# Four gate products of the feed-forward moved across a step boundary in a macaron block

## The chip, the cores and the metric

The kernel runs on one core of one Trainium2 chip. The metric is the device time of one execution in microseconds; the median of several executions is compared. A profile of one execution is read beside it. PE is TensorE, PEld its weight loads, DVE is VectorE, ACT is ScalarE, POOL is GpSimd and SP is SyncE, which issues nearly all DMAs.

## The reference

A macaron block over x of shape (4, 1024, 512): half a feed-forward, a selective-scan layer, half a feed-forward with the same weights, each on a layer norm of its input and added to it.

```python
x = x + 0.5 * ffn(layernorm(x))
x = x + attn(layernorm(x))
x = x + 0.5 * ffn(layernorm(x))

def ffn(x):                       # gate_w, up_w: 1408 x 512, down_w: 512 x 1408
    g = (x @ gate_w.T) * gate_s
    u = (x @ up_w.T) * up_s
    return (silu(g) * u) @ down_w.T * down_s

def attn(x):                      # 1024 channels, 16 states each
    h, gate = split(W_in @ x.T)
    h = silu(conv4(h) + conv_b)
    ts, Bm, Cm = split(h.T @ Wx.T)          # 128, 16, 16; each rms-normed
    delta = softplus(Wdt @ ts + dt_bias)
    # per channel and state: s = exp(delta * A) * s + delta * B * h;  y = sum_n s * C
    return ((y + D * h) * silu(gate)) @ Wout.T
```

All arithmetic is float32.

## The kernel before

The 4096 rows of x are 32 tiles of 128 rows. The scan layer works in sixteen steps, k = 0 to 15, of 256 positions (two tiles). Four steps make one of the four sequences. Beside the scan of a step, its "background" does three other things: a feed-forward over three or four row tiles (some of the first feed-forward, some of the second, by the table BESIDE), the output projection of the step before, and the input projection, convolution and scan parameters of the step after. A front part before step 0 and an end part after step 15 do the rest.

The numbers of tiles by step are 3, 3, 4, 4, 3, 4, 4, 3, 4, 4, 3, 4, 4, 3, 3, 3. So a step with three is followed by a step with four at k = 1, 4, 7 and 10.

**The scan.** A step has 32 units, `unit(k, i, g)`: eight channel blocks i by four groups g of states. "Unit i" of a step is written below for the four groups of block i. In a unit, ACT computes exponentials into PSUM (`da`, L573, two instructions for each of two halves), POOL the product with B (`sb`, L576), DVE the recurrence (L580) and the product with C (L590). PE sums over the states with a folding matrix (`yps`, L602), one block later; these sums free the 14 buffers of `sb`. The exponentials use `rep`, a copy of delta and delta times h that is spread over partitions through two DMAs (`rows`, `spread`). Before a pair of blocks, `head` computes delta: PE forms `dp` (L490), ACT takes its absolute value, relu, exponential and logarithm (`z`, `lg`, L498 to L503), and POOL completes `dd`. Its parts are popped as "chores" inside the units.

**The feed-forward of a step.** `FFN.flip` transposes a normalised tile on PE (`tpf`, L235) and ACT copies it to `fxT` (L238). `gate()` has eleven parts; a part has four matmuls against one 256 KB weight tile (`gate_w`, L273) and a copy to `hd` on ACT (L287). After parts 3, 7 and 10 a silu runs over the copies so far (L199), with a load of its function table ahead of it and another after it. `up()` has eleven parts of the same matmuls, which DVE multiplies into `hd` (L304). `down()` has one part for each tile, eleven matmuls of 512 columns (`fo`, L319), which DVE adds to the tile (`xf`, L327). `hd` and `fxT` have one buffer each.

**The order.** `background(k)` (L704) writes the parts in a list: loads, statistics, then gate and up parts as a rhythm between which the gate projection of the scan (`gp`, L545), transposes, the output projection (`op`, L633), the convolution (`hp`, L376) and the parameters (`sp`, `t`, then `tsT`, L455) stand, and at the end the transposes of the next step's feed-forward between the down parts. Each part is a `Work` with a cost for PE and one for DVE. The main loop emits a unit and then as many parts as keep the shares of both costs level with the units (`total` and `total_v` are sums over the step's list):

```python
while parts and (
    done * total_v < vector * total
    or (length - len(parts)) * (units - HEAD) < upto * min(n, units - HEAD)
):
    c, v = step()
    done, vector = done + c, vector + v
```

The second condition has the parameters of the next step ready eleven units before the end (HEAD). A scheduler may still reorder instructions a little when the program is built, except where the code pins the order.

Weight tiles are fetched in the order of the parts, twelve ahead (LEAD), into a ring of fourteen; all of them and the scan's DMAs go through SP's queue.

Of the kernel before, what the change touches and what calls it, by code (L numbers as in the profile page):

```python
# [25 lines left out]
NCS = B * CPB  # L26
# [7 lines left out]
HALVES = 14  # L34
LEAD = 12
FRONT = 5
RING = 14

BESIDE = [(3, 0), (3, 0), (2, 2), (2, 2), (1, 2), (2, 2), (2, 2), (2, 1), (2, 2), (2, 2), (2, 1), (2, 2), (2, 2), (1, 2), (0, 3), (0, 3)]
# [3 lines left out]
def macaron_kernel(ctx: ExitStack, tc: tile.TileContext, a: dict, out: bass.AP):  # L43
# [8 lines left out]
    p8 = ctx.enter_context(tc.tile_pool(name="p8", bufs=8))  # L52
    ring = ctx.enter_context(tc.tile_pool(name="ring", bufs=RING))
    dram = ctx.enter_context(tc.tile_pool(name="scratch", bufs=1, space=bass.MemoryType.DRAM))
# [109 lines left out]
    def settle():  # L164
        while deferred:
            deferred.pop(0)[1]()
# [20 lines left out]
    def then(f, *args):  # L187
        return Work(0, 0, lambda: f(*args))
# [54 lines left out]
    class FFN:  # L243
# [35 lines left out]
        def gate(self):  # L279
            self.done = 0  # L280

            def part(it):
                def emit(w):
                    if it == 0:
                        self.hd = p1.tile([P, NF, 2 * T], F32, tag="hd", name=f"hd{self.name}")
                    gp = self.product("gate_w", it, w[0])
                    nc.scalar.activation(  # L287
                        self.hd[:, it, : self.n], gp, AF.Copy, scale=gate_s[:, it : it + 1]
                    )
                    if it % 4 == 3 or it == NF - 1:  # L290
                        h = self.hd[:, self.done : it + 1, : self.n]
                        silu(h)
                        self.done = it + 1

                return Work(KH * self.n, 0, emit, [("gate_w", it)], settled=it == 0)

            return [part(it) for it in range(NF)]
# [69 lines left out]
    def prep_conv(k):  # L367
        def part(i):
            def emit(w):
                if i == 0:  # L370
                    st[k]["u"] = p2.tile([P, NI, T], F32, tag="u", name=f"u{k}")
                u = st[k]["u"]
                hp = ps_m.tile([P, 512], F32, tag="mm", name=f"hp{k}_{i}")
                w = cols(w[0])
                for kk in range(KH):
                    nc.tensor.matmul(  # L376
                        hp[:, : K - 1 + T], lhsT=w[:, kk, :], rhs=st[k]["xnT"][:, kk, :],
                        start=(kk == 0), stop=(kk == KH - 1),
                    )
                nc.scalar.activation(  # L380
                    u[:, i, :], hp[:, 0:T], AF.Identity,
                    bias=conv_b[:, i : i + 1], scale=conv_w[:, i, 0:1],
                )

                def taps():
                    for q in range(1, K):
                        pin(nc.vector.scalar_tensor_tensor(  # L387
                            u[:, i, :], hp[:, q : q + T], conv_w[:, i, q : q + 1], u[:, i, :],
                            ALU.mult, ALU.add,
                        ))  # L390
                    if i == NI - 1:
                        defer(1, lambda: silu(u))

                defer(1, taps)

            return Work(KH * T, 4 * T, emit, [("W_in", i)], settled=i == 0)

        return [part(i) for i in range(NI)]
# [223 lines left out]
    def tail(k):  # L622

        wo = []

        def part(j):
            def emit(w=None):
                wo.extend(w or [])
                assert all(("gated", i) in st[k] for i in range(NI))
                x = st[k]["xo", j]  # L630
                op = ps_m.tile([P, H], F32, tag="mm", name=f"op{k}_{j}")
                for i in range(NI):
                    nc.tensor.matmul(  # L633
                        op, lhsT=st[k]["u"][:, i, j * P : (j + 1) * P], rhs=wo[i],
                        start=(i == 0), stop=(i == NI - 1),
                    )
                nc.vector.tensor_tensor(x, x, op, ALU.add)
                if k + 1 < NCS:
                    store(x2[k * J + j], x)

            return Work(NI * H, H, emit, [("Wout", i) for i in range(NI)] if j == 0 else (), settled=j == 0)

        r = [part(j) for j in range(J)]
        r[0].until = r[-1]
        return r

    def weave(xs, by):

        r = []
        for n, w in enumerate(xs):  # L650
            r.append(w)
            r += by[n : n + 1]
        return r, by[len(xs) :]

    def flips(f, prep):

        seq = [(f, t) for t in range(len(f.tiles))] if f else []
        if prep is not None:
            seq += [(None, j) for j in range(J)]
        xn = {}  # L660

        def begin(n):
            if n < len(seq):
                of, t = seq[n]
                xn[n] = of.stats(t) if of else prep_stats(prep, t)

        def start():
            begin(0)
            begin(1)

        def part(n):
            def emit():
                of, t = seq[n]
                if of:
                    of.flip(xn[n], t)
                else:
                    prep_flip(prep, t, xn[n])
                begin(n + 2)

            return Work(KH * P, H if n + 2 < len(seq) else 0, emit)  # L680

        return [Work(0, 2 * H, start)] + [part(n) for n in range(len(seq))]
# [13 lines left out]
    ffn = {k: FFN(k, beside[k]) for k in range(NCS)}  # L696
# [7 lines left out]
    def background(k):  # L704

        f = ffn[k]
        prep = k + 1 if k + 1 < NCS else None
        gates, out_of = gate(k), tail(k - 1) if k else []
        turn = flips(None, prep) if prep is not None else []
        conv = params = []  # L710
        if prep is not None:
            conv, params = prep_conv(prep), prep_params(prep)
            ready[k] = params[-1]
        parts = [then(tail_load, k - 1)] if k else []
        if prep is not None:
            parts.append(then(prep_load, k + 1))
        parts += turn[:1]
        p = [NOTHING] * (4 if k else 0) + gates + turn[1:] + out_of + conv
        tiles = (f.gate() if k else []) + f.up()
        p = [p[n : n + 2] for n in range(0, len(p), 2)]  # L720
        p += [[NOTHING]] * 4 + [[w] for w in params]
        turn = flips(ffn[k + 1], None) if k + 1 < NCS else []
        for n, w in enumerate(tiles):
            parts.append(w)
            for q in p[n : n + 1]:
                parts += q
            if n == len(tiles) - NF and k + 1 < NCS:
                parts.append(then(ffn[k + 1].load))
            if n == len(tiles) - NF and k + 1 == NCS:
                parts.append(then(tail_load, k))  # L730
                parts.append(then(end_load))
            if n == len(tiles) - 2:
                parts += turn[:1]
        for q in p[len(tiles):]:
            parts += q
        w, turn = weave(turn[1:2] + f.down(), [NOTHING] + turn[2:])
        return parts + w + turn

    ready = {}


# [5 lines left out]
    front += [turn_f[0]] + weave(prep_conv(0), [down[3]] + turn_f[1:])[0]  # L747
    front += weave(gate_0[:FRONT], prep_params(0))[0]
    beside_scan = [background(k) for k in range(NCS)]
    end = FFN("e", last)  # L750
    turn = flips(end, None)
    back_end = tail(NCS - 1) + turn + end.gate() + end.up() + end.down()
    for w in front + gate_0[FRONT:] + [w for b in beside_scan for w in b] + back_end:
        if w.blocks:
# [8 lines left out]
    settle()  # L763
    between = gate_0[FRONT:]
    chores = head(0, 0)
# [16 lines left out]
    for k in range(NCS):  # L782
        more = k + 1 < NCS
        parts, n, done, vector = list(beside_scan[k]), 0, 0, 0
# [121 lines left out]
```

## Time and profile before

| | us |
|---|---|
| median of 3 executions | 3239.61 (3236.33 to 3240.49) |
| the profiled execution | 3238.13 |
| its span, first to last instruction | 3236.4 |
| front part, to the first exponential of step 0 | 200.5 |
| steps 1, 4, 7, 10 (three tiles, before four) | 192.7, 175.9, 178.7, 186.2 |
| steps 2, 5, 8, 11 (four tiles, after three) | 183.1, 182.4, 181.6, 181.9 |
| steps 3, 6, 9, 12 (four tiles, after four) | 185.0, 186.2, 186.3, 186.2 |
| end part, from the end of step 15's scan | 134.4 |

A page of the profile gives the busy time of each engine, groups of equal instructions, and the chain of work that ended last. Each view can be asked for a window of the span. The table cuts the span where the first exponential of a step starts on ACT; PE and DVE may be a little ahead of or behind this cut. In a line, "out<-in" are tiles by their names in the program, "x" is a count of instructions, and a bracket has the idle time before it and who ended it. A float32 matmul appears as two records, so a gate product of four matmuls has eight. PEclk is the granted share of PE's clock.

### The profile page before, as it was taken

The numbers are of one execution on the slowest core, as the hardware profiler recorded it, in microseconds if no ns is written. First come the engines' busy times: TensorE is split into PE (matmuls) and PEld (weight loads), VectorE is DVE, ScalarE is ACT, GpSimd is POOL, SyncE is SP. The second block draws the span as 40 slices with busy tenths as digits, with TensorE's granted clock in tenths as the row PEclk, the third lists the DMA queues.
The fourth block names the chain that finished last, engine by engine and source line by source line (L and its number), as shares of the span: only waits on it lengthen the run. The fifth ranks groups of instructions, "written<-read, shape, count | busy, mean of one in ns | idle before, by whom it ended". The sixth has DMA issues, their size and how long they took to land.

```text
span 3236.4 us, 41939 instructions
## 1 busy us (share of the span) xinstructions
PE 3057.3 (94%) x12448; PEld 1648.5 (51%) x12448; DVE 2475.0 (76%) x4981; ACT 1787.2 (55%) x3535; POOL 1937.9 (60%) x1895
## 2 busy tenths in 40 slices
PE   8988898999999999999999999989999998989999
PEld 3554453545555454545545554645555554554434
DVE  1259788888969898787979798787969788788831
ACT  3265564747556664746565564747556474655430
POOL 0066857566675757566765767576665756667510
PEclk9999998999999999999999999999999999999999
DMA  5364554646566555546565655655565654646531
GB/s 169 113 170 118 172 171 135 178 120 199 138 186 175 171 167 160 171 122 209 136 180 163 182 157 162 187 133 171 153 177 162 172 171 135 179 117 195 143 97 43
DMA packets 287426, 506.43 MB, mean 156 GB/s; under 512 B 32096, under 2 KB 50272, under 8 KB 287200
## 3 DMA queue, kind: packets, MB, share of 16 engines
q1 hardware_dynamic: 285616, 503.31, 54.7%
q8 instruction: 100, 1.64, 0.2%
q14 instruction: 126, 1.03, 0.1%
q10 hardware_dynamic: 1584, 0.45, 0.1%
HBM read 442.03 MB, written 61.60 MB: 156 GB/s over the span
## 4 chain that ended last, share of the span: by engine, by line
PE 61%; DVE 20%; ACT 8%; POOL 5%; issue 4%; DMA 1%; SPq 0%; ACTq 0%; DVEq 0%; POOLq 0%
PE fo L319 13%; PE gate_w L273 12%; DVE da L580 12%; PE up_w L273 7%; PE hp L376 5%; PE yps L602 5%; PE gp L545 5%; PE op L633 4%; DVE sb L590 4%; ACT da L573 3%; POOL sb L576 2%; PE gate_wp L273 1%; PE dp L490 1%; PE gate_we L273 1%; PE foe L319 1%
## 5 line engine op out<-in xcount | busy, mean ns | idle before, releaser
L576 POOL TENSOR_TENSOR sb<-rep,bc 128x512 f32<-128x512 f32 x1024 | 1275.4, 1273 | 450.1 <-PE yps L602 378.5
L580 DVE TENSOR_TENSOR_SCAN da<-da,state,sb 128x256 f32<-128x256 f32 x1536 | 1055.9, 737 | 284.4 <-ACT da L573 250.3
L573 ACT ACTIVATE da<-rep,a_w 128x256 f32<-128x256 f32 x2048 | 899.1, 471 | 537.3 <-DVE sb L590 521.7
L590 DVE TENSOR_TENSOR sb<-da,bc 128x512 f32<-128x512 f32 x1024 | 686.1, 677 | 0.9
L273 PE MATMUL gate_w<-fxT,w_gate_w 128*128 128x384 f32 (+1 forms) x1408 | 565.8, 549 | 5.6 <-ACT dd L499 2.3
L273 PE MATMUL up_w<-fxT,w_up_w 128*128 128x384 f32 (+1 forms) x1408 | 564.5, 551 | 0.8 <-issue 0.4
L319 PE MATMUL fo<-w_down_w,hd 128*128 128x512 f32 x1232 | 546.5, 598 | 0.0
L602 PE MATMUL yps<-sb,fold 128*32 128x256 f32 x4096 | 320.0, 393 | 84.0 <-DVE sb L590 75.3
L273 PEld LDWEIGHTS up_w<-fxT,w_up_w 128*128 128x128 f32 x1408 | 267.0, 194 | 249.5 <-issue 157.1
L273 PEld LDWEIGHTS gate_w<-fxT,w_gate_w 128*128 128x128 f32 x1408 | 267.3, 193 | 247.0 <-issue 151.3
L580 DVE TENSOR_TENSOR_SCAN da<-da,sb 128x256 f32<-128x256 f32 x512 | 320.4, 677 | 85.4 <-ACT da L573 66.0
L319 PEld LDWEIGHTS fo<-w_down_w,hd 128*128 128x128 f32 x1232 | 231.4, 192 | 273.1 <-issue 264.0
L521 POOL TENSOR_SCALAR e<-z 128x512 f32<-128x512 f32 x64 | 124.3, 1942 | 276.1 <-ACT z L502 252.1
L602 PEld LDWEIGHTS yps<-sb,fold 128*32 128x32 f32 x4096 | 125.9, 110 | 281.3 <-DVE sb L590 133.5
L376 PE MATMUL hp<-mxT,w_W_in 128*128 128x259 f32 x1024 | 243.6, 390 | 24.4 <-issue 13.0
L545 PE MATMUL gp<-mxT,w_W_in 128*128 128x256 f32 x1024 | 241.3, 385 | 2.9 <-ACT dd L499 1.8
L376 PEld LDWEIGHTS hp<-mxT,w_W_in 128*128 128x128 f32 x1024 | 193.9, 192 | 82.8 <-issue 34.2
L633 PE MATMUL op<-w_Wout,u 128*128 128x512 f32 x512 | 225.0, 595 | 4.6 <-issue 2.9
L545 PEld LDWEIGHTS gp<-mxT,w_W_in 128*128 128x128 f32 x1024 | 193.6, 191 | 60.7 <-issue 17.9
L287 ACT ACTIVATE hd<-gate_w,gate_s 128x384 f32<-128x384 f32 (+1 forms) x176 | 110.5, 629 | 166.2 <-PE gate_w L273 165.3
L387 DVE SCALAR_TENSOR_TENSOR u<-hp,conv_w,u 128x256 f32<-128x256 f32 x384 | 177.1, 473 | 17.4 <-ACT u L380 14.6
L304 DVE SCALAR_TENSOR_TENSOR hd<-up_w,up_s,hd 128x384 f32<-128x384 f32 (+1 forms) x176 | 117.2, 666 | 59.9 <-PE up_w L273 59.8
(112 smaller groups left out, 2654.2 us busy)
## 6 DMA issues: line engine op xcount, KB each, us to landing
rep<-row SPq DMA_DIRECT2D x512, 256.0 KB, 5.1
w_W_in<-in_W_in_dram SPq DMA_DIRECT2D x256, 256.0 KB, 3.4
w_gate_w<-in_gate_w_dram SPq DMA_DIRECT2D x198, 256.0 KB, 3.9
w_up_w<-in_up_w_dram SPq DMA_DIRECT2D x198, 256.0 KB, 3.2
w_down_w<-down_w SPq DMA_DIRECT2D x187, 256.0 KB, 2.8
row<-dd SPq DMA_DIRECT2D x128, 256.0 KB, 3.2
w_Wout<-in_Wout_dram SPq DMA_DIRECT2D x128, 256.0 KB, 3.4
bc<-bcd SPq DMA_DIRECT2D x64, 256.0 KB, 4.7
```

Source lines behind the costliest of these rows:

```text
L273: nc.tensor.matmul(o[:, : self.n], lhsT=w[:, k, :], rhs=self.xT[:, k, : self.n], start=(k == 0), stop=(k == KH - 1),)
L319: nc.tensor.matmul(op, lhsT=self.hd[:, it, t * P : (t + 1) * P], rhs=wd[it], start=(it == 0), stop=(it == NF - 1),)
L376: nc.tensor.matmul(hp[:, : K - 1 + T], lhsT=w[:, kk, :], rhs=st[k]["xnT"][:, kk, :], start=(kk == 0), stop=(kk == KH - 1),)
L387: pin(nc.vector.scalar_tensor_tensor(u[:, i, :], hp[:, q : q + T], conv_w[:, i, q : q + 1], u[:, i, :], ALU.mult, ALU.add,))
L521: lambda: pin(nc.gpsimd.tensor_scalar(e, z, 1.0, 1.0, ALU.add, ALU.subtract)),
L545: nc.tensor.matmul(gp[:, :T], lhsT=w[:, kk, :], rhs=st[k]["xnT"][:, kk, K - 1 :], start=(kk == 0), stop=(kk == KH - 1),)
L573: nc.scalar.activation(da[:, j, :], rep[:, h + j, 0, :], AF.Exp, scale=a_w[:, b0 + h + j, g : g + 1])
L576: nc.gpsimd.tensor_tensor(sb, rep[:, hs, 1, :], d["bc"][:, g : g + 1, :].to_broadcast([P, 2, T]), ALU.mult)
L580: nc.vector.tensor_tensor_scan(da[:, j, :], da[:, j, :], sb[:, j, :], 0.0 if first else state[:, b0 + h + j, g : g + 1], ALU.mult, ALU.add,)
L590: nc.vector.tensor_tensor(sb, da, d["bc"][:, NS + g : NS + g + 1, :].to_broadcast([P, 2, T]), ALU.mult)
L602: nc.tensor.matmul(yp[j * Q : (j + 1) * Q, :], lhsT=fold, rhs=pr[j // 2][:, j % 2, :], start=(g == 0), stop=(g == NS - 1),)
L633: nc.tensor.matmul(op, lhsT=st[k]["u"][:, i, j * P : (j + 1) * P], rhs=wo[i], start=(i == 0), stop=(i == NI - 1),)
```

## The change

At the end of the list of step k, if step k has fewer feed-forward tiles than step k+1, the first four gate parts of step k+1 are appended; step k+1 starts with the other seven. This holds at k = 1, 4, 7 and 10. Step 0 and the last are left out by the condition. The moved parts are the same instructions with the same weight loads; the costs that the planner sums up move with them from one step to the other.

```diff
+EARLY = 4
...
     def background(k):
...
-        tiles = (f.gate() if k else []) + f.up()
+        tiles = (begun.pop(k) if k in begun else f.gate() if k else []) + f.up()
...
         w, turn = weave(turn[1:2] + f.down(), [NOTHING] + turn[2:])
-        return parts + w + turn
-
+        parts += w + turn
+        if 0 < k < NCS - 1 and len(f.tiles) < len(ffn[k + 1].tiles):
+            gates = ffn[k + 1].gate()
+            parts += gates[:EARLY]
+            begun[k + 1] = gates[EARLY:]
+        return parts
+
+    begun = {}
     ready = {}
```

## The prediction, made before the changed kernel ran

> **What bounds the kernel now.** I read the page's busy times first, then cut the span into the sixteen scan steps (a step has 128 of the 2048 exponentials of L573; it starts with its first), then followed the chain of waits through steps 4 and 5, then the waits behind it.
>
> Busy times on the page:
>
> ```profile
> PE 3057.3 (94%) x12448; PEld 1648.5 (51%) x12448; DVE 2475.0 (76%) x4981; ACT 1787.2 (55%) x3535; POOL 1937.9 (60%) x1895
> ```
>
> The windows of steps 4, 5, 10 and 11 (start:end us, length, then busy us and instructions of PE, PEld, DVE, ACT, POOL, then PEclk, the DMA share and GB/s):
>
> ```profile
> 914.20:1090.10 175.90, 167.12 (x777) 97.67 (x775) 146.61 (x325) 110.00 (x224) 122.49 (x119) 0.99 0.65 184
> 1090.10:1272.50 182.40, 176.96 (x715) 94.38 (x716) 155.56 (x323) 107.52 (x214) 120.49 (x119) 0.99 0.55 154
> ...
> 2005.30:2191.50 186.20, 171.11 (x775) 98.50 (x773) 154.52 (x328) 110.89 (x224) 121.66 (x119) 0.96 0.61 173
> 2191.50:2373.40 181.90, 176.80 (x714) 94.28 (x715) 152.97 (x262) 107.43 (x214) 119.70 (x119) 0.98 0.55 154
> ```
>
> PE is nearly always busy, yet the steps with three tiles (4, 10) are not shorter by the work that they lack. Window minus PE busy gives PE's idle time: 8.8 and 15.1 us in steps 4 and 10, 5.4 and 5.1 in the four-tile steps after them. The same sum for all eight steps that the change touches (1, 2, 4, 5, 7, 8, 10, 11) is 22.3+5.6+8.8+5.4+10.8+3.7+15.1+5.1 = 76.8 us. DVE is idle for 26 to 39 us in each of them. Neither engine is the bound alone.
>
> The chain of waits through steps 4 and 5 (start, us, what) shows who has it when:
>
> ```profile
> 1040.99 1.84 DVE da L580 x3
> ...
> 1052.87 9.44 PE fo L319 x22
> ...
> 1075.79 9.44 PE fo L319 x22
> 1085.24 0.88 PE dp L490 x4
> 1086.14 0.47 ACT z L498
> ...
> 1090.51 1.86 DVE da L580 x3
> 1092.43 0.59 DVE sb L590
> 1093.07 1.73 PE yps L602 x8
> 1094.80 11.33 PE gate_w L273 x24
> ...
> 1109.58 3.43 PE gate_w L273 x8
> ```
>
> In the middle of a three-tile step the chain is vector work (DVE, with ACT and POOL); from the down products on it is PE; at the end it drops to ACT and DVE for 8 us; then it is PE again, through gate, op, hp and up products to 1221 us. So a three-tile step has a stretch where PE has spare time, and the step after it is bound by PE through its first 130 us. The drop at the end is seen in the timelines of ACT and DVE, and of PE (last: idle before, and who ended it):
>
> ```profile
> 1086.14 0.47 ACT L498 ACTIVATE z<-dp,dt_b 128x256 f32<-128x256 f32 x1 [8.13 <-PE dp L490]
> ...
> 1113.06 0.69 ACT L287 ACTIVATE hd<-gate_w,gate_s 128x512 f32<-128x512 f32 x1 [3.06 <-PE gate_w L273]
> ```
>
> ```profile
> 1089.61 0.70 DVE L580 TENSOR_TENSOR_SCAN da<-da,sb 128x256 f32<-128x256 f32 x1 [4.61 <-ACT da L573]
> ...
> 1119.92 0.76 DVE L580 TENSOR_TENSOR_SCAN da<-da,state,sb 128x256 f32<-128x256 f32 x1 [8.28 <-ACT da L573]
> ```
>
> ```profile
> 1093.07 1.73 PE L602 MATMUL yps<-sb,fold 128*32 128x256 f32 x8 [5.10 <-DVE sb L590]
> ```
>
> ACT's z stands in its queue ahead of the last unit's exponentials and waits for a dp product that PE has behind the last down product; DVE starves for 4.6 us, and PE then waits 5.1 us for the last sums. In the next step DVE starves for 8.3 us, because the copy of the fourth gate product and its silu stand in ACT's queue ahead of unit 1's exponentials.
>
> **What the Trainium skill says.** "TensorE: Matmul & The Clock Gate", Part 1, says that ACT and DVE take their queues strictly in order; the waits above agree. The same part says that PE's clock falls to half after an idle window of some 3.4 us. The trace agrees: PEclk is 0.96 in step 10, and its three gate products after a 5.28 us wait took 11.85 us where three at full clock take 10.29. "ScalarE: Activation LUTs", What ACT_TABLE_LOAD costs, gives 1283 ns for a load; the groups of ACT have 1283 ns too. "Perfetto Trace Analysis", Optimization Strategy, says that where the most-contended engine changes over time, interleaving the regimes can help; the chain above is such a case, and no run here shows the gain yet.
>
> **The change part by part.** A gate product of four tiles costs PE 3.43 us (the chain's x8 row). The condition holds for steps 1, 4, 7 and 10 (three tiles, four in the next): sixteen products, 54.9 us of PE work, change place; none is added or removed. Their sixteen weight loads (256 KB, 3.9 us to landing) keep their place in the order of work, and the ring still runs twelve loads ahead, so I put DMA at nothing; the xo and xi loads of the next step now come behind them on SP, but both are first read a unit later (stm at 1110, issued at 1095): nothing, and some 5 us a step if that cover fails. The four copies to hd (0.69 us) and one batch of silu (two table loads of 1.28 and 1.91 us) move with them on ACT. hd and fxT have one buffer each; the down products that read the old hd and the transposes that write fxT precede the gates on PE anyway, so these waits are short: nothing, up to 1 us a step.
>
> The planner counts the four products in the three-tile step, so all its parts come earlier against the units, and fewer stand in the next. In the built order of PE the last up product and the first down product now precede the sums of unit 5, where they followed; dp of the next step's first head comes behind ten matmuls of the first down product; the last down product precedes the sums of unit 6; the four gates stand in front of the sums of unit 7; and dp of the second head stands between gates two and three, with ACT's z behind all of unit 7's exponentials.
>
> (a) Before the down products. PE waited 2.54 us for tsT at dp in step 4 (3.19 in step 7) and ran the next 3.4 us at half clock, 1.7 us lost. The first down product now fills this: r = 4.2 us earlier in step 4 (2.54+1.7), about 5 in step 7; 4 taken for all, bounds 0 and 6.
>
> (b) At the step's end. The z wait goes, and the gates cover the last sums. With PE's work in its new order, the first gate starts 1.9+0.6 us (sums of unit 6, a transpose) after the last down product: in step 4 at 1085.9-r, and not at 1094.8. Sums of unit 7 follow four gates and a dp, 15 us later, by when DVE is done. PE has gained 5.1 us, 1.3 us of slow clock, and r: 10 us. In step 10, where PE waited 3.06, 2.76 and 5.28 us in this stretch, it gains about 20.
>
> (c) What is late next. The batch of silu now stands ahead of unit 0 of the next step, not unit 1. ACT needs 0.69+1.28+1.91+1.28 = 5.2 us from the fourth gate: its start+14.6+5.2 = 19.8, while DVE ended unit 7 at about 8.5, so DVE starves some 11.5 us there. The second batch (gates 4 to 7, PE at +33.6) is ready at +39, when DVE has done unit 0 (four groups of 4.1 us) and the statistics: no wait. Before unit 2 now stand all eleven gates, where seven stood, and the silu of g: some 7 us more. Starved in all 19 us, against 4.6+8.3 and, in DVE's timeline just ahead of and within unit 2, 3.3+1.3: 17.5. With its start at 1085.9-r, unit 2 runs effectively from 1149.7-r and not 1141: DVE is about 5 us later there, although PE is 10 us ahead.
>
> (d) After that DVE is full to the end of the up products. It makes up 2.3 us of small stalls. The built order also puts tsT's copy one and a half groups earlier on DVE (6 us, less one hd product of 0.7): dp and the down products start at 8.6-4-2.3-5.5, 3 us earlier than before. The last up product, 3.4 us, used to follow this dp and now precedes it. The four down products that end the step are PE's: 6.6 us gained for steps 4 and 5. By the same sums, step 10 with 4.7 us of z wait gone, unit 0 starting about when it did and unit 2 0.6 us earlier, gives 0.6+1.5+5.5+3.4, 11 us; step 1 has the same waits, 11; step 7 has slow clock of 6.8 us at its end, 8.
>
> Sum 6.6+8+11+11 = 36.6, of which I take 35. The profiled execution took 3238.13 us, 1.73 more than its span: 3238.1-35 = 3203. The median of the runs shown is 1.5 above it: 3205.
>
> **Rivals.**
> (1) A wait in place of the one removed, slower. The silu batches rule step k+1: eleven gates instead of seven (13.7 us) stand ahead of its unit 2 on ACT, and if r is nothing and tsT comes no earlier, each pair ends 8.6-2.3 = 6 us later, 25 in all: 3264. It decides once DVE's starved time between the last unit and unit 2 exceeds the 17.5 us of before by more than PE's saved waits return. For it: (c) has DVE late by 5 us. Against: (d), the later part is fuller on PE before than after.
> (2) Work is only exchanged. Step 4 grows to a four-tile step's 182 us and step 5 falls to 176: the sum stays, 3240. For it: DVE has 147 to 156 us in either. Against: PE waits and slow clock at the boundary are seen to go.
> (3) All of PE's idle time in the eight steps is recovered: 3240-77 = 3163. For it: 54.9 us of work fit in it. Against: DVE is full for 65 us before the step's end.
> That the change does nothing is excluded by the built order.
>
> **How the numbers follow.** Main case 0.60, from 20 to 58 us gained (r from 0 to 6, (d) whole or in half); (2) 0.14; (1) 0.17; (3) 0.09. The range leaves out (3) and most of (1): 3180 to 3243. About 0.2%, 6.5 us, is what a measurement can tell from no change. Faster takes the main case, (3) and a third of (2): 0.74. Same takes half of (2) and a little of (1): 0.08. Slower: 0.18.
>
> **What would show it.** In the new profile: no wait of some 5 us of yps for sb and no half clock at the ends of steps 1, 4, 7 and 10; z for dp gone there; dp for tsT, 32.6 us in fifteen waits, lower by about 11. DVE's wait of 11 us between the steps shows (c). Steps 4 and 10 keep their length within some 6 us and steps 5 and 11 shrink by 6 to 14. It is wrong if steps 5 and 11 keep their 182 us, or if rep or xi loads end waits of POOL or DVE there.

## The result, and the profile after

The changed kernel takes 3262.99 us in the median (3262.39 to 3264.71, 4 runs). The kernel before took 3240.05 us beside it (3236.33 to 3240.88, 4 runs). The ratio is 1.0074, with a 95% interval of 1.0063 to 1.0086: 23 us slower, where 35 us of gain were forecast. The time is that of rival (1), which gave 3264; whether for rival (1)'s reason is asked below. The profiled execution has a span of 3261.8 us against 3236.4, at a granted clock no lower (0.981 and 0.977), so the clock is not what lengthened it.

Busy times on the page of the changed kernel:

```profile
PE 3065.9 (94%) x12448; PEld 1643.3 (50%) x12448; DVE 2472.3 (76%) x4981; ACT 1790.0 (55%) x3534; POOL 1936.4 (59%) x1895
```

No engine works longer by more than 9 us, so most of the loss is waiting. The chain of work that ended last says who is waited for; its shares of the span on the page of the changed kernel, then of the kernel before:

```profile
PE 50%; DVE 26%; ACT 9%; issue 6%; POOL 6%; DMA 2%; SPq 0%; ACTq 0%; DVEq 0%; POOLq 0%
```

```profile
PE 61%; DVE 20%; ACT 8%; POOL 5%; issue 4%; DMA 1%; SPq 0%; ACTq 0%; DVEq 0%; POOLq 0%
```

Where the loss lies is seen in windows of the changed kernel: steps 4, 5 and 6, then steps 1 to 12 together (start:end us, length, busy us of PE, PEld, DVE, ACT, POOL, then PEclk, DMA share, GB/s).

```profile
911.60:1100.00 188.40, 184.51 (x825) 104.97 (x824) 151.13 (x333) 118.33 (x232) 130.05 (x126) 1.00 0.69 193
1100.00:1283.70 183.70, 173.84 (x716) 91.22 (x717) 156.27 (x324) 102.35 (x212) 111.67 (x112) 0.97 0.52 147
1283.70:1468.00 184.30, 177.04 (x711) 93.48 (x711) 151.14 (x313) 106.34 (x211) 120.90 (x116) 0.99 0.53 149
...
351.30:2582.80 2231.50, 2133.84 (x8928) 1153.29 (x8929) 1834.30 (x3697) 1303.46 (x2604) 1445.92 (x1404) 0.99 0.57 161
```

The same windows of the kernel before, for step 6 and for steps 1 to 12:

```profile
1272.50:1458.70 186.20, 184.40 (x754) 97.19 (x753) 156.72 (x324) 107.80 (x216) 120.32 (x116) 1.00 0.57 162
...
353.40:2559.60 2206.20, 2122.66 (x8926) 1158.45 (x8927) 1836.83 (x3697) 1300.59 (x2605) 1446.82 (x1404) 0.98 0.58 163
```

Steps 1 to 12 grew from 2206.2 to 2231.5 us. Window minus busy gives PE's idle time. In step 4 it fell from 8.8 to 3.9 us, but in step 5 it rose from 5.4 to 9.9 and in step 6, which the change doesn't touch, from 1.8 to 7.3. Over the twelve steps it rose from 83.5 to 97.7 us, and PE's busy time by 11.2 us with the same products, which no run explains. DVE's busy time hardly changed, so its idle time, from 369.4 to 397.2 us, is only the loss over again; that more of the kernel now goes by DVE's pace is what the chain says. The four places are not alike: step 1 and the two steps behind it changed by -0.7 us in all, step 4 and its two by +12.1, step 7 by +7.0, step 10 by +6.8.

PE at the end of step 4 does what was forecast. Its timeline in the changed kernel:

```profile
1076.94 1.93 PE L603 MATMUL yps<-sb,fold 128*32 128x256 f32 x32
1078.81 0.66 PE L236 MATMUL tpf<-ident,xnf 128*128 128x128 f32 x4
1080.14 7.13 PE L274 MATMUL gate_w<-fxT,w_gate_w 128*128 128x512 f32 x16 [0.67 <-ACT fxT L239]
1087.11 1.03 PE L491 MATMUL dp<-tsT,w_dt 128*128 128x256 f32 x4
1087.97 7.03 PE L274 MATMUL gate_w<-fxT,w_gate_w 128*128 128x512 f32 x16
1094.93 1.93 PE L603 MATMUL yps<-sb,fold 128*32 128x256 f32 x32
```

The 5.10 us wait of the sums is gone, four gate products are done by 1095, and dp stands between the second and the third. DVE, in the same stretch and the next 50 us, does not follow; its waits of over a microsecond are these:

```profile
1101.64 2.68 DVE L581 TENSOR_TENSOR_SCAN da<-da,state,sb 128x256 f32<-128x256 f32 x4 [8.85 <-POOL dd L512]
1120.89 1.55 DVE L581 TENSOR_TENSOR_SCAN da<-da,state,sb 128x256 f32<-128x256 f32 x2 [1.59 <-ACT da L574]
1147.20 0.75 DVE L305 SCALAR_TENSOR_TENSOR hd<-up_w,up_s,hd 128x512 f32<-128x512 f32 x1 [9.54 <-PE up_w L274]
```

Two of ACT's stretches lie beside them, ahead of units 0 and 2:

```profile
1095.04 0.69 ACT L288 ACTIVATE hd<-gate_w,gate_s 128x512 f32<-128x512 f32 x1 [2.75 <-PE gate_w L274]
1095.74 1.28 ACT L200 ACT_TABLE_LOAD   x1
1097.04 1.91 ACT L200 ACTIVATE hd<-hd 128x2048 f32<-128x2048 f32 x1
1098.97 1.28 ACT L201 ACT_TABLE_LOAD   x1
1100.26 1.67 ACT L574 ACTIVATE da<-rep,a_w 128x256 f32<-128x256 f32 x4
...
1137.84 1.28 ACT L200 ACT_TABLE_LOAD   x1
1139.13 1.91 ACT L200 ACTIVATE g<-g 128x2048 f32<-128x2048 f32 x1
1141.06 1.28 ACT L201 ACT_TABLE_LOAD   x1
...
1143.42 1.28 ACT L200 ACT_TABLE_LOAD   x1
1144.72 1.48 ACT L200 ACTIVATE hd<-hd 128x1536 f32<-128x1536 f32 x1
1146.22 1.28 ACT L201 ACT_TABLE_LOAD   x1
1147.52 1.67 ACT L574 ACTIVATE da<-rep,a_w 128x256 f32<-128x256 f32 x4
```

Ahead of unit 0 stand the copy of the fourth product and a silu with its two loads. Ahead of unit 2 stand the silu of the scan's gate and the last silu of the feed-forward, 9.7 us with a copy and one exponential between them. DVE's queue has at the same place the multiply of the first up product, so the trace names PE there; but the exponentials of unit 2 come no earlier than 1147.5 either. At the first wait the trace names POOL, whose `dd` ended at the same moment; at the same place of steps 2, 8 and 11 it names ACT (6.88, 8.34 and 6.88 us), and the run with a joined silu below shows which of the two it was.

Among the waits of the whole trace, one rose and one fell as the order was changed. The changed kernel, then the kernel before (us, times, longest):

```profile
ACT z L499 <- PE dp L491: 113.8, 41, 8.8
...
PE dp L491 <- DVE tsT L456: 18.8, 7, 3.4
```

```profile
ACT z L498 <- PE dp L490: 86.8, 35, 8.9
...
PE dp L490 <- DVE tsT L455: 32.6, 15, 3.9
```

PE no longer waits so long for tsT. But ACT waits 27 us more for dp. One such place is the end of step 5, where dp stands behind the last down product and the `z` now stands ahead of step 6's first exponentials: in ACT's and DVE's timelines of the changed kernel,

```profile
1281.27 0.47 ACT L499 ACTIVATE z<-dp,dt_b 128x256 f32<-128x256 f32 x1 [6.12 <-PE dp L491]
```

```profile
1285.28 0.76 DVE L581 TENSOR_TENSOR_SCAN da<-da,state,sb 128x256 f32<-128x256 f32 x1 [4.60 <-ACT da L574]
```

In the kernel before, DVE has no wait there. The wait that was removed from the end of step 4 stands, at the same 4.6 us of DVE, one step later.

### The profile page after: what moved, and what is told of

Same layout as the page of the kernel before. It is cut to its first block, busy times and chain, and to the rows that moved or that the text cites. A ratio compares the mean times of both kernels' runs of the same rounds, so it can differ in the third digit from the quotient of the medians.

```text
span 3261.8 us, 41947 instructions
## 1 busy us (share of the span) xinstructions
PE 3065.9 (94%) x12448; PEld 1643.3 (50%) x12448; DVE 2472.3 (76%) x4981; ACT 1790.0 (55%) x3534; POOL 1936.4 (59%) x1895
## 4 chain that ended last, share of the span: by engine, by line
PE 50%; DVE 26%; ACT 9%; issue 6%; POOL 6%; DMA 2%; SPq 0%; ACTq 0%; DVEq 0%; POOLq 0%
DVE da L581 16%; PE fo L320 12%; PE gate_w L274 9%; DVE sb L591 5%; PE up_w L274 5%; PE yps L603 4%; PE hp L377 4%; PE gp L546 4%; PE op L634 3%; POOL sb L577 3%; ACT da L574 2%; DVE u L388 1%; PE dp L491 1%; DVE hd L305 1%; PE gate_wp L274 1%
## 5 line engine op out<-in xcount | busy, mean ns | idle before, releaser
L546 PEld LDWEIGHTS gp<-mxT,w_W_in 128*128 128x128 f32 x1024 | 193.1, 190 | 52.0 <-issue 12.9
```

The lines of the kernel that those rows point to most:

```text
L546: nc.tensor.matmul(gp[:, :T], lhsT=w[:, kk, :], rhs=st[k]["xnT"][:, kk, K - 1 :], start=(kk == 0), stop=(kk == KH - 1),)
```

## The experiments

Theory A, at the start, was that all eleven gate products and the silu of the scan's gate now stand ahead of unit 2; B that the planner overfills the three-tile step; C that a silu batch stands ahead of unit 0 in ACT's queue. Later theories are put where they come up. A row that doesn't say "before" is a variant of the changed kernel, but for the planner's sums.

Each run has its ratio to the kernel before and the length of steps 1 to 12 in its trace, which leaves out the front and the last steps; before it is 2206.2 us, in the changed kernel 2231.5.

| run | ratio (95%) | steps 1 to 12 |
|---|---|---|
| three products moved | 1.0053 (1.0038 to 1.0068) | 2219.1 |
| silu joined in four steps | 1.0003 (0.9995 to 1.0012) | 2215.4 |
| planner's sums alone | 1.0014 (1.0008 to 1.0021) | 2208.2 |
| move without the sums | 1.0107 (1.0092 to 1.0123) | 2238.6 |
| before, joined in four steps | 1.0002 (0.9994 to 1.0010) | 2206.9 |
| before, joined everywhere | 1.0023 (1.0014 to 1.0032) | 2216.6 |
| silu placed later | 1.0091 (1.0077 to 1.0105) | 2238.2 |
| joined everywhere | 1.0016 (1.0009 to 1.0022) | 2216.1 |
| scan parts earlier | 1.0058 (1.0043 to 1.0073) | 2223.5 |
| before, scan parts earlier | 1.0136 (1.0121 to 1.0151) | 2248.1 |
| products cut | 1.0044 (1.0029 to 1.0059) | 2220.8 |
| before, products cut | 1.0071 (1.0054 to 1.0088) | 2229.0 |
| no silu | 1.0006 (0.9997 to 1.0015) | 2205.4 |
| before, no silu | 1.0010 (1.0001 to 1.0019) | 2206.5 |
| one boundary | 1.0042 (1.0027 to 1.0057) | 2216.7 |
| joined, and scan parts earlier | 1.0057 (1.0042 to 1.0072) | 2226.5 |
| one silu in four steps | 1.0016 (1.0008 to 1.0024) | 2212.0 |

**Size of the move, and the planner's part.** Three products in place of four, so that the program moves no silu with them:

```diff
-EARLY = 4
+EARLY = 3
```

> Three gate products are moved and not four, so the first silu and its two table loads stay behind unit 0 of the next step. Theory A (all eleven gate products and the silu of g now stand ahead of the next step's unit 2, on PE and so on ACT): ten or eleven products still stand ahead of unit 2, so most of the loss stays, ratio to before about 1.005. Theory B (the three-tile step is filled too full by the planner): three quarters of the loss, 1.0055. Theory C (the silu batch ahead of unit 0 on ACT holds the vector work): half of the loss or more goes, at most 1.003, and DVE's wait of 8.8 us at the first exponentials of steps 2, 5, 8 and 11 goes.

The loss halved, to 12.9 us, and the ratio of 1.0053 is near theory A's figure and B's. But the run did not do what it was for. ACT's timeline ahead of step 5, and DVE's:

```profile
1097.89 1.91 ACT L200 ACTIVATE hd<-hd 128x2048 f32<-128x2048 f32 x1
...
1101.11 1.67 ACT L574 ACTIVATE da<-rep,a_w 128x256 f32<-128x256 f32 x4
```

```profile
1102.49 2.68 DVE L581 TENSOR_TENSOR_SCAN da<-da,state,sb 128x256 f32<-128x256 f32 x4 [11.02 <-POOL sb L577]
```

The scheduler put the fourth product and its silu ahead of unit 0 all the same, and DVE waited longer there than with four. So this run says nothing against theory C.

The planner's sums changed as by the move, with no product moved; and the products moved with the old sums (the other way round):

```diff
+        if k in filled:
+            total += EARLY * KH * ffn[k + 1].n
```

> No product is moved. The planner's PE total of steps 1, 4, 7 and 10 is raised by the cost of four gate products, as in the changed kernel, so that their parts come earlier against the units. Theory A: no loss; the waits at the end of these steps shrink, ratio 0.996 to 1.000. Theory B: the loss is here, 1.004 to 1.007. Theory C: as A.

> Four products are moved to the end of steps 1, 4, 7 and 10, but the planner's total of these steps is kept as it was before, so that the products come in one block between the steps; step k+1 has seven gate parts and a smaller total, as in the changed kernel. Theory A: the loss is here, 1.006 to 1.012. Theory B: little loss, at most 1.002. Theory C: a loss like the changed kernel's, 1.006 to 1.009.

The planner's earlier order alone costs 2 us over the twelve steps. Without it the move costs 32 us. So the planner is not what makes it slow (theory B falls). In the run without it no silu stands ahead of unit 0 (the first table load begins 11.6 us after step 5's first exponential), and it is slower still, so theory C can't be the whole.

**The silu.** In the four steps that begin with moved products, the silu over columns 0 to 3 runs with that over 4 to 7:

```diff
-                    if it % 4 == 3 or it == NF - 1:
+                    if (it % 4 == 3 and not (it == 3 and self.begun)) or it == NF - 1:
```

> Four products are moved; the silu of these four columns of hd is joined with that of the next four, so no table load stands ahead of unit 0. Theory C: the loss falls to 1.002 or below and the 8.8 us wait shrinks to about 4. Theory A: the wait goes, but unit 2 still waits for the eleventh gate product and two silus; 1.005 to 1.007. Theory B: no change, 1.007.

16 of the 25 us of steps 1 to 12 come back. DVE's timeline of this run, from unit 0 to unit 2:

```profile
1093.10 2.68 DVE L582 TENSOR_TENSOR_SCAN da<-da,state,sb 128x256 f32<-128x256 f32 x4 [4.19 <-ACT da L575]
1098.59 2.68 DVE L582 TENSOR_TENSOR_SCAN da<-da,state,sb 128x256 f32<-128x256 f32 x4 [1.50 <-ACT da L575]
1120.11 2.68 DVE L582 TENSOR_TENSOR_SCAN da<-da,state,sb 128x256 f32<-128x256 f32 x4 [7.73 <-ACT da L575]
1142.03 0.75 DVE L306 SCALAR_TENSOR_TENSOR hd<-up_w,up_s,hd 128x512 f32<-128x512 f32 x1 [5.86 <-PE up_w L275]
```

The first wait went from 8.85 to 4.19 us by taking the batch out. POOL's `dd` ended at 1097.75 here, after DVE had begun: it was ACT. What is left of it is the copy of the fourth product. But the wait at unit 1 grew to 7.73 us; the four sum to 19.3 us where the changed kernel has 20.0, and unit 2 began only 1.2 us sooner after step 4's first exponential. Where the 16 us come from is taken up below. The ratio of 1.0003 flatters this run: 10 us of it are from step 13, which took 187.7 us before and 177.4 here, and which no edit touches; the scheduler had built its order on ACT and DVE a little otherwise. This is why the twelve steps are compared.

Two things went with that batch, its place ahead of unit 0 and its two loads. So the same edit was made in the kernel before, where the silu stands at another place, and in the changed kernel the batch was kept but issued behind the sixth copy:

```diff
+                    late = self.name in (2, 5, 8, 11)
-                    if it % 4 == 3 or it == NF - 1:
-                        h = self.hd[:, self.done : it + 1, : self.n]
+                    if (it % 4 == 3 and not (late and it == 3)) or it == NF - 1 or (late and it == 5):
+                        top = 4 if it == 5 else it + 1
+                        h = self.hd[:, self.done : top, : self.n]
```

> The kernel before, with one thing taken from the joined-silu run: in steps 2, 5, 8 and 11 the silu of columns 0 to 3 runs together with that of columns 4 to 7. Theory C (it is the place of the silu ahead of unit 0, not the number of silu batches, that the joined run took away): without the move there is nothing to take away, ratio 0.999 to 1.001. Rival N (one batch of silu less, with two table loads of 1.28 us, frees ACT some 6 us in each of four steps whatever its place, and the move still costs its 0.7%): ratio 0.993 to 0.996.

> The changed kernel with as many batches of silu as it has, but in steps 2, 5, 8 and 11 the one over columns 0 to 3 is issued behind the copy of the sixth gate product, not behind that of the fourth; it so stands behind exponentials of unit 0 and no longer ahead of them. Theory C (place): the loss goes although no table load goes, ratio to before 0.999 to 1.003. Rival N (number of table loads): ratio as that of the change, 1.006 to 1.009.

Neither theory holds as it was put. In the kernel before a batch less gains nothing (against N), and in the changed kernel a later place gains nothing (against C). DVE's timeline of the run with the later place shows why:

```profile
1100.85 2.68 DVE L583 TENSOR_TENSOR_SCAN da<-da,state,sb 128x256 f32<-128x256 f32 x4 [4.19 <-ACT da L576]
1106.70 2.68 DVE L583 TENSOR_TENSOR_SCAN da<-da,state,sb 128x256 f32<-128x256 f32 x4 [1.86 <-ACT da L576]
1115.00 2.68 DVE L583 TENSOR_TENSOR_SCAN da<-da,state,sb 128x256 f32<-128x256 f32 x4 [3.93 <-POOL sb L579]
```

4.19, 1.86 and 3.93 us stand where 8.85 and 1.59 stood: the batch stops ACT for its 4.5 us wherever it is, and DVE has no stock of exponentials to bridge that. That it counts in the changed kernel and not in the kernel before was then theory S; its test leaves the silu of the gate out in steps 2, 5, 8 and 11, in both kernels:

```diff
-                    if it % 4 == 3 or it == NF - 1:
+                    if (it % 4 == 3 or it == NF - 1) and self.name not in (2, 5, 8, 11):
```

> The changed kernel without the silu of the gate in the four feed-forwards of steps 2, 5, 8 and 11 (all three batches with their table loads, some 4.5 us of ACT each, are left out; copies and products stay). To be read against the run beside it, which leaves the same out of the kernel before. Theory S (the move loses because silu batches, which wait in ACT's queue for PE's products, stand ahead of the exponentials of units 0 and 2): without them the move gains what PE saved, so this run is 10 to 35 us faster than the run beside it. Rival O (the loss is in the built order as a whole and not in the silu): it stays 15 to 30 us slower than the run beside it.

> The kernel before without the silu of the gate in the feed-forwards of steps 2, 5, 8 and 11, the same part left out. DVE waits 8.3 and some 4 us behind the first two batches in step 5; with four such steps, 20 to 50 us gained: ratio 0.985 to 0.994. It is the base for the run beside it.

Windows of steps 1 to 12 of the changed kernel without silu, then of the kernel before without silu, with its step 5 behind:

```profile
352.70:2558.10 2205.40, 2126.64 (x8928) 1155.85 (x8929) 1832.22 (x3697) 1253.78 (x2568) 1447.24 (x1404) 0.99 0.58 163
```

```profile
353.20:2559.70 2206.50, 2123.46 (x8926) 1158.47 (x8927) 1835.00 (x3697) 1251.74 (x2569) 1446.05 (x1404) 0.98 0.58 163
...
1090.10:1272.40 182.30, 176.88 (x715) 94.33 (x716) 155.26 (x323) 95.05 (x205) 120.27 (x119) 0.99 0.55 154
```

ACT loses 49 us of work in the kernel before, and its twelve steps change by 0.3 us, where 20 to 50 us of gain were expected; step 5 has 182.3 us, as with silu, and PE's products stand in the same order. In the changed kernel the same edit takes 26.1 us off. The move costs 25.3 us with the silu and -1.1 without. The scheduler built another order there too, so not every microsecond of this is the silu's own; but counted from step k's first exponential, unit 2 of step k+1 begins 6.0, 6.7, 4.1 and 6.3 us earlier without it at the four places (k = 1, 4, 7, 10), and at most 0.4 earlier or later in the kernel before. Without the move the silu costs nothing; with it, most of 26 us.

Theory S expected a gain of 10 us or more once the silu was gone, and there is none. The reason is seen if PE's time is cut at the end of the last down product of each step, which gives one stretch a step. That of step 6 begins and ends with these lines, in the changed kernel, then in the kernel before:

```profile
1270.77 9.61 PE L320 MATMUL fo<-w_down_w,hd 128*128 128x512 f32 x22
...
1463.75 9.71 PE L320 MATMUL fo<-w_down_w,hd 128*128 128x512 f32 x22
```

```profile
1268.68 9.61 PE L319 MATMUL fo<-w_down_w,hd 128*128 128x512 f32 x22
...
1454.41 9.71 PE L319 MATMUL fo<-w_down_w,hd 128*128 128x512 f32 x22
```

From end to end that is 193.1 us against 185.8. The change of these stretches against the kernel before, each summed over the four places, in us (the matmuls of a stretch are the same in all these runs, but for one block of sums, under 2 us, which goes from step k to step k+1 where the planner's sums are changed):

| run | step k | step k+1 | step k+2 | sum |
|---|---|---|---|---|
| the changed kernel | -47.7 | +41.5 | +30.8 | +24.6 |
| planner's sums alone | -48.7 | +50.3 | +0.4 | +2.0 |
| silu joined in four steps | -47.5 | +41.6 | +14.4 | +8.5 |
| no silu | -45.4 | +19.0 | +25.1 | -1.3 |
| scan parts earlier (below) | -47.7 | +69.6 | -4.7 | +17.2 |
| before, no silu | +0.4 | -0.2 | +0.1 | +0.3 |

PE's early end of step k comes of the planner's sums. With the silu, step k+1 gives nearly all of it back; without it, 26.4 us are still won there. Then step k+2, in which no product is moved and no silu left out, takes 25 to 31 us. So there are two losses of about the same size: the silu on ACT in step k+1, and one in step k+2. The second goes with the place of the displaced `z`. Where it stands ahead of step k+2's first exponentials, as in eleven of eighteen runs (the changed kernel among them, and one with a single place), step k+2 is longer, by 4.6 to 40.4 us; where it stands behind them, as in the other seven and in the kernel before, it changes by -4.7 to +2.1. No run moves `z` alone, so this is a sorting of runs and not yet a proof. The 16 us of the joined silu all come from step k+2, where nothing was joined: they are the built order's and can't be credited to the silu.

**PE's work and order.** The sixteen moved products were cut to a quarter of their matmuls, in the changed kernel and, where they stand, in the kernel before:

```diff
+            kh = 1 if name == "gate_w" and it < 4 and self.name in (2, 5, 8, 11) else KH
-            for k in range(KH):
+            for k in range(kh):
```

> The changed kernel, with the sixteen moved gate products cut to one of their four matmuls; left out are three of the four blocks of 128 input columns in columns 0 to 511 of the gate of the four feed-forwards, 41 us of PE work at 3.43 us a product. Copies, silu, order and planner costs stay. Theory V: PE has time to spare there and the vector stream sets the end, so the time hardly falls: 0 to 10 us against the changed kernel, ratio to before 1.004 to 1.008. Rival (PE's products ahead of unit 2 set it): 25 to 41 us, ratio 0.995 to 1.000.

> The kernel before with the same sixteen products cut to one of four matmuls where they stand, at the start of steps 2, 5, 8 and 11; the same part of the gate is left out. It measures what PE's work there is worth before the change. If PE bounds the first 130 us of such a step, as the prediction had it: 25 to 41 us gained, ratio 0.987 to 0.992. Theory V: 0 to 12 us, ratio 0.996 to 1.000.

The products left out are 41 us at 3.43 us each; PE's busy time in steps 1 to 12 fell by 12.7 us only, and by 13.0 in the kernel before. The twelve steps of the changed kernel gained 10.7 us, about the most of theory V's 0 to 10, and the kernel before became 24 us slower, which neither theory held possible. DVE's timeline of the latter, early in step 5, and the eighth copy and its silu on ACT, ahead of unit 2:

```profile
1123.72 2.68 DVE L581 TENSOR_TENSOR_SCAN da<-da,state,sb 128x256 f32<-128x256 f32 x4 [8.85 <-ACT da L574]
1152.67 2.68 DVE L581 TENSOR_TENSOR_SCAN da<-da,state,sb 128x256 f32<-128x256 f32 x4 [11.51 <-ACT da L574]
```

```profile
1146.08 0.69 ACT L288 ACTIVATE hd<-gate_w,gate_s 128x512 f32<-128x512 f32 x1 [4.26 <-PE gate_w L274]
1146.79 1.28 ACT L199 ACT_TABLE_LOAD   x1
1148.08 1.91 ACT L199 ACTIVATE hd<-hd 128x2048 f32<-128x2048 f32 x1
```

In the kernel before the exponentials of unit 2 stood ahead of the eighth copy and its silu. Here the scheduler, given shorter products, put both ahead of unit 2, and DVE waited 11.51 us. The planner's costs and the program's order were kept. So this run measures ACT's order more than PE's work, and it can't be read as a price of PE work.

The list pairs scan parts with feed-forward products by count: with four moved, `op` stood behind eight more, and PE reached it 236.3 us after step 4's first exponential instead of 228.3. A shift by four entries in steps 2, 5, 8 and 11 takes that back, in the changed kernel and as a control in the kernel before:

```diff
+        if k in (2, 5, 8, 11):
+            for q in p[:4]:
+                parts += q
+            p = p[4:]
```

> The changed kernel, but in steps 2, 5, 8 and 11 the first four entries of the list of scan parts (two empty ones and four of the eight gp products) are put ahead of the feed-forward products, so that op, hp and the parameters stand behind four feed-forward products of this step and not behind eight. Theory P (the list pairs scan parts with feed-forward products by count, so with four of them moved op still stood behind eight more, twelve in all, and what PE had gained was spent ahead of op; the parameters then came 2 us later, not earlier): op is reached some 12 us earlier, the wait for t goes, ratio to before 0.992 to 1.001. Rival V (ACT's queue and DVE set these steps, whatever PE's order): 1.005 to 1.010.

> The kernel before, with the same shift of the scan parts in steps 2, 5, 8 and 11 and nothing moved across the step: op behind four feed-forward products and not behind eight. The control for the run beside it. Theory P: PE has no lead to spend here, and the products taken from ahead of op stand later in the step: ratio 0.998 to 1.006. If it is as fast as the run beside it, the shift alone did it and the move is worth nothing.

`op` came at 225.0 us, 11.3 earlier than in the changed kernel, but only 8 us of the 25 came back; theory P falls as the main cause. The control is a miss: 44 us slower than the kernel before (1.0136, where 0.998 to 1.006 were expected), for a reason that was not followed up. With the shift in both kernels the move is the faster by 24.6 us. So what the move costs is not one number: it depends on the order that it is put into, and the silu alone does not make it a loss.

**One boundary, and candidates.** The change from step 4 to step 5 alone (the condition is `k == 4`):

> The change at one boundary only, from step 4 to step 5. In the changed kernel the steps 4 to 6 together took 12.1 us more than before and steps 7 to 9 and 10 to 12 7 each. If each pair pays for itself: 8 to 14 us slower, ratio 1.0025 to 1.0043, and steps 7 to 13 as before within 2 us. If the pairs pay for one another through the order that the scheduler builds: steps without the change differ by more than that.

13 us slower; steps 4 to 6 took 555.8 us against 544.5, and steps 7 to 12 are as before within 0.5 us each. This boundary pays for itself: 11.3 us alone, 12.1 beside the other three.

Candidates: two batches in every feed-forward, without and with the move; the shift with the joined silu; and one silu over all eleven columns in steps 2, 5, 8 and 11.

```diff
-                    if it % 4 == 3 or it == NF - 1:
+                    if it == 7 or it == NF - 1:
```

> The kernel before, with two batches of silu of g (columns 0 to 7, 8 to 10) in place of three in every feed-forward. Theory C: ACT's queue has one block less in sixteen steps, but it is where DVE starves 8.3 us behind the copy of the fourth product; the second batch is then the longer: 0.996 to 1.001. Rival N: 24 us and more gained, ratio 0.975 to 0.993.

> The changed kernel with two batches of silu of g in every feed-forward. Theory C: against the joined run of four steps (1.0003) only the other twelve steps change, as in the kernel before with all joined; ratio to before 0.996 to 1.002. Rival N: 0.975 to 0.993.

> A candidate: the changed kernel with the scan parts four products earlier in steps 2, 5, 8 and 11 and with the silu of columns 0 to 3 joined to that of 4 to 7 there. The first took 0.17% off the changed kernel, the second 0.7%. If these add: ratio to before 0.997 to 1.001. If the order built anew undoes it: 1.002 to 1.008.

```diff
+                    if (it % 4 == 3 and self.name not in (2, 5, 8, 11)) or it == NF - 1:
```

> A candidate: the changed kernel with one silu of g over all eleven columns behind the last gate product in steps 2, 5, 8 and 11, in place of three. Theory S: two of three batches are out of ACT's queue ahead of unit 2 and nothing is left out; the run without any silu gave 1.0006 and the one with the first batch joined 1.0003, so 0.998 to 1.003, unless the last batch, 128 x 5632 and some 5 us long just ahead of unit 2, holds DVE there as long as the two before it did: then 1.003 to 1.006. It does not beat the kernel before by more than 0.2%.

None beats the kernel before. With two batches everywhere the move costs nothing (2216.1 against 2216.6 us), which agrees with the pair without silu; but there the kernel before lost 10.4 us by the edit, and why is open. The shift and the joined silu do not add; the order built anew undid it.

## Why the prediction was wrong

- **The bound.** That "the step after it is bound by PE through its first 130 us" fits the kernel before: PE is idle for 5.4 of step 5's 182.4 us, and leaving the silu out changes nothing. After the move DVE starves 20.0 of the 55 us between unit 7 of step 4 and unit 2 of step 5, and the chain passes from PE, which holds it from 1117 to 1138 us, to ACT's two silus until 1147.5 and then to DVE. The Trainium skill ("Perfetto Trace Analysis", Optimization Strategy) was cited for it that interleaving regimes may help; here it put waits for ACT in place of waits of PE, and no run with the move beats the kernel before.
- **(a) and (b), PE.** Right for the end of step 4. The first gate started 168.5 us after step 4's first exponential, where 1085.9 - 4 - 914.2 = 167.7 were forecast. dp's wait for tsT fell by 13.8 us where 11 were named. The sums' wait at the step's end is gone, and PEclk is 1.00 in steps 4 and 10.
- **(c), the silu batches.** The mechanism was right and its sum near: DVE starved 20.0 us between the last unit and unit 2, where 19 were forecast. The parts were off, 8.85 where 11.5 were forecast at unit 0, and 9.54 where 7 were ahead of unit 2. Yet unit 2 of step 5 began 236.3 us after step 4's first exponential against 225.6 before: 10.7 us late, and not 5. (At the other three places unit 2 was 0.9 us early, 6.1 late and 1.0 late.) 6.3 of these 10.7 are there at unit 7 already. That dp would come behind ten matmuls of the first down product was seen, and put at nothing; but POOL waited for its `z`, and DVE lost 4.4 us ahead of and in unit 6, mostly to POOL's `sb` behind it, where before it lost 0.2. POOL's timeline in the changed kernel:

```profile
1055.85 1.95 POOL L522 TENSOR_SCALAR e<-z 128x512 f32<-128x512 f32 x1 [5.51 <-ACT z L503]
```

- **(d), the recovery.** This is the step that failed: "The four down products that end the step are PE's: 6.6 us gained for steps 4 and 5", and by the same sums 11, 8 and 11. At the last down product of step k+1, 4.8 us were lost in steps 4 and 5; 7.9, 0.3 and 2.8 were gained at the other three: 6.2 us in place of 36.6. The silu is the larger part of what is missing, for without it 26.4 us are gained there. The shift of tsT's copy was sized rightly: dp was 5.1 us late where unit 2 had been 10.7. The 2.3 us of small stalls were not made up; unit 6 was 12.3 us late, and PE waited 4.86 us for `sn` ahead of t. And the sum ended there: the step behind, k+2, was put at nothing without a reason, and lost 7.3, 7.3, 7.3 and 9.0 us, with `z` ahead of its exponentials. The sign of failure that the prediction named came: steps 5 and 11 took 183.7 and 184.4 us where they were to shrink by 6 to 14.
- **Rival (1)** named the place and the total (25 us), and the run without silu supports its cause. But its sum was 6 us at each pair, from an r of nothing and a tsT no earlier. PE's first gate came 12 us earlier, tsT did come earlier against the units, and the four places cost -0.7, 12.1, 7.0 and 6.8 us, most of it in step k+2, of which it says nothing. By its own measure, DVE's starved time between the last unit and unit 2, it was 2.5 us over the 17.5. That its 3264 was met within 1 us is luck. It was given too little because (d) was counted as its counterweight.
- **Rival (2)**, work only exchanged, has the sum that is left with the silu out of the way (-1.1 us), by a gain and a loss of some 26 us each. Rival (3) fell: PE's idle time grew.
- **DMA, hd and fxT** were put at nothing. The waits of DVE's `stm` for xi, a unit late in the queue, are as before (3.7 us in all against 3.8). POOL's waits for rep rose from 39.8 to 56.3 us, one of the marks of failure that were named; one of 5.92 us lies at this boundary, but its `sb` ended at 1089.7 and DVE's scan began at 1101.64, so DVE did not wait for it there.

What stays open: whether the place of `z` is all that costs 25 to 31 us in step k+2, and why half of that is left where one batch was joined a step earlier. Each edit also changes the order that the scheduler builds, by as much as 10 us in a step that the edit doesn't touch, and runs a few us apart can't be told from that. Neither an exponential pinned ahead of the silu nor a `z` pinned behind the exponentials of step k+2 was tried.

## What to carry to other kernels

Before work is moved off the bounding engine, ask for each helper engine what its instructions wait for at the new place: here the four matmuls brought a copy and a silu with two table loads into ACT's queue ahead of the exponentials that DVE lives on. A wait that costs nothing while another engine is the bound can cost nearly all of itself once that engine is ahead; count the new state's waits, not the old one's. And carry the sum past the last step that is changed: a gain that an engine has at the end of one step can be lost in the next, which holds the same work in another order.

## What the runs showed that was not expected

- A silu batch of four columns holds ACT for 4.5 us, 1.28 + 1.91 + 1.28, in the trace. The Trainium skill ("ScalarE: Activation LUTs", What ACT_TABLE_LOAD costs) gives about 1283 ns for a load, and both loads are seen here; the drain of about 1380 ns that it adds is not seen, for the silu starts 0.02 us behind the load. Leaving 49 us of such work out changed the twelve steps of the kernel before by 0.3 us, and those of the changed kernel by 26.1.
- Cutting PE work made a kernel slower, by 0.71%: with products planned shorter, the scheduler placed instructions of ACT that wait for PE ahead of those that DVE needs.
- The same step 13, untouched by any edit, took 177.4 us in one run and 187.7 in another, with its order built a little otherwise.
- Four steps that the change leaves as they are, 3, 6, 9 and 12, with the same matmuls, took 30.8 us more; they did so in every run that had `z` ahead of their first exponentials, by differing amounts.
